# Layer 3 of a four-layer network: who empties the score banks, VectorE alone or ScalarE and VectorE crosswise

## The chip, the cores and the metric

The kernel runs on one core of one Trainium2 chip. The metric is the device time of one execution in microseconds; less is better. Five engines work side by side, each through its own queue in order: TensorE (PE, with its weight loads shown as PEld), VectorE (DVE), ScalarE (ACT), GpSimd (POOL) and SyncE (SP), which issues most of the DMAs.

## The reference

The input is `x`, 4 images of 256 channels and 48 x 48 pixels in fp32. Four layers follow each other, each a residual layer on a group norm: `x = x + layer(gn(x))`. Layer 0 is a 7x7 dilated attention, layers 1 and 2 are 3x3 convolutions with quantized weights. Layer 3, the one that is changed, is a linear attention with three window sizes:

```python
# x stands for gn(x) here
q = sigmoid(Wq x); k = sigmoid(Wk x); v = normalized(Wv x)      # 8 heads of 32 channels
Ikv = integral(k v^T)                                          # running sums over rows and columns
for w in (1, 2, 4):
    wkv = box(Ikv, 48 // w)                                    # sum over a window around each pixel
    attn = (q . wkv) / (q . box(integral(k), 48 // w) + 1e-6)
out = Wout concat(attn for each w) + bout
```

For each pixel and head, then, the products of `q` with the `k` of all pixels in a window of 48, 24 or 12 pixels a side weight the `v` of these pixels.

## The kernel before, in words

The kernel computes layer 3 as sums over masked scores. Image `b`, half of the heads `ct` (4 heads, two pairs) and a stripe of 8 rows of queries `rb` make a block; there are 4 x 2 x 6 = 48 blocks. Keys come in tiles of 8 rows by 16 columns, so that 128 keys fill the partitions: row stripe `a`, column group `c` of 3. `tiles_of(rb)` lists the tiles that the widest window reaches: those up to three stripes away. The half sizes of the three windows are `HALVES` = 24, 12 and 6, numbered `wi` = 0, 1, 2.

For each tile and each of the two pairs, `scores` has TensorE multiply 128 keys with the queries that the widest window can reach, into a tile `s` of two PSUM banks. `ps_s` holds two such tiles, one for each pair, so the next tile's scores of a pair wait until this tile's are read. `masked` then turns scores into up to three pieces in an SBUF tile `sm`, one for each window, each multiplied by a 0/1 mask (bf16, `masks`). `sums` multiplies the pieces with `v` and adds them up in the accumulators `acc`, one for each window; it runs two tiles later (`LAG = 2`), after that tile's scores. Pool `smp` has six `sm` tiles, two for each of three tiles of keys.

What `masked` does depends on how many stripes lie between keys and queries:

- Up to one stripe (`full` and `many` hold; a *near* tile, 384 of 720): the widest window covers whole columns, which `whole` adds from precomputed sums, so that only strips at its sides are masked (`pieces[0]`: one of 16 columns or two of 8). The middle window's piece (`wi` 1) is 27, 28 or 39 columns of 8 rows for two heads: 432, 448 or 624 elements per partition. VectorE multiplies strips and middle straight from PSUM. GpSimd makes the smallest window's piece out of the middle piece, in SBUF.
- Two stripes (`full`, not `many`; 192 tiles): the strips as above by VectorE; ScalarE copies the 3 or 4 rows of the middle piece to SBUF, and GpSimd masks it there in place. The two engines go crosswise: ScalarE copies the second pair while VectorE reads the first, then they change over.
- Three stripes (not `full`; 144 tiles): only the widest window reaches, and VectorE multiplies the whole piece, 560 to 768 elements, from PSUM for both pairs.

`tiles_of` takes near and far tiles in turn. The main loop's order is written out by hand and kept (`InOrder`): scores of tile n, its masking, the sums of tile n - 2, then `advance()`, which lets the background jobs take a step: the projections of the next image (`Projection`), the running sums for the norms (`k_sums`), the norms (`norms`), the states of the keys (`state`, `window_state`), and loading and finishing of blocks (`prepare`, `finish`). These put work on all engines between two tiles. Most instructions are recorded through one helper, so the profile gives them one line, L143, and they are told apart by the names of their tiles.

The order of masking before is this, with `first` and `second` the two pairs; of `copy` and `middle` at most one does something for a given tile:

```python
copy(*second)
middle(*first)
widest(*first)
copy(*first)
middle(*second)
widest(*second)
```

Of the kernel before, what the change touches and what calls it, by code (L numbers as in the profile page):

```python
# [146 lines left out]
def conv_preact_kernel(  # L147
# [53 lines left out]
    pe, dve, act, pool, sync = (  # L201
        InOrder(tc, e) for e in (nc.tensor, nc.vector, nc.scalar, nc.gpsimd, nc.sync)
    )
# [249 lines left out]
    with (  # L453
# [479 lines left out]
        def load_row(pool_, tag, a):  # L933

            t = pool_.tile([P, NCT, K0, P], F32, tag=tag, name="wrow")
            sync.dma_start(
                out=t, in_=w1[:, a * K0 : (a + 1) * K0, :].rearrange("(ct p) k o -> p ct k o", p=P)
            )
            return t
# [442 lines left out]
        with tc.tile_pool(name="wst", bufs=1) as wst:  # L1382
            for ct in range(NCT):
                fetch_x(0, ct)
            rows = [load_row(k1p, "k1", 0), load_row(vp, "v", MT), load_row(vp, "v", MT - 1)]
# [43 lines left out]
        with (  # L1429
# [11 lines left out]
            first = ExitStack()  # L1441
# [41 lines left out]
    with (  # L1483
# [243 lines left out]
        def rows_seen(wi, a, rb):  # L1727

            h = HALVES[wi]
            return (  # L1730
                max(0, a * RB - h + 1 - rb * RB),
                min(RB, a * RB + RB + h - rb * RB),
            )

        def cols_seen(wi, c):
            h = HALVES[wi]
            return max(0, c * KC - h + (wi > 0)), min(W, c * KC + KC + h)

        def rows_whole(a, rb):

            return abs(a - rb) * RB + RB <= HALVES[0]
# [5 lines left out]
        def strips(c):  # L1747

            (c0, c1), (f0, f1) = cols_seen(0, c), cols_whole(c)
            return [(p0, p1) for p0, p1 in ((c0, f0), (f1, c1)) if p0 < p1]  # L1750

        class Block:
# [28 lines left out]
            def masked(self, a, c, ss):  # L1781

                rb = self.rb
                all0 = rows_seen(0, a, rb), cols_seen(0, c)
                (r0, r1), (c0, c1) = all0
                wis = [wi for wi in range(NW) if seen(wi, a, rb)]
                full = rows_whole(a, rb)
                pieces = {wi: [cols_seen(wi, c)] for wi in wis}
                if full:
                    pieces[0] = strips(c)  # L1790

                def room():

                    t = smp.tile([P, SM_ROOM], F32, tag="sm", name="sm")
                    at, got = 0, {}
                    for wi in wis:
                        nr = rows_seen(wi, a, rb)[1] - rows_seen(wi, a, rb)[0]
                        for p0, p1 in pieces[wi]:
                            n = 2 * nr * (p1 - p0)
                            got[wi, p0] = t[:, at : at + n].rearrange(  # L1800
                                "p (j r w) -> p j r w", j=2, r=nr
                            )
                            at += n
                    assert at <= SM_ROOM
                    return got

                pairs = [room() for _ in ss]

                def view(tiles, wi, rows, cols):
                    y0, _ = rows_seen(wi, a, rb)  # L1810
                    x0 = next(p0 for p0, p1 in pieces[wi] if p0 <= cols[0] and cols[1] <= p1)
                    return tiles[wi, x0][
                        :, :, rows[0] - y0 : rows[1] - y0, cols[0] - x0 : cols[1] - x0
                    ]

                def times_mask(engine, wi, rows, cols, dst, src):
                    mr = rb * RB + rows[0] - (a * RB - HALVES[wi] + 1)
                    mc = cols[0] - (c * KC - MCOL0[wi])
                    nr, ncol = rows[1] - rows[0], cols[1] - cols[0]
                    m = mask[wi][:, mr : mr + nr, mc : mc + ncol]  # L1820
                    engine.tensor_mul(
                        dst, src, m.unsqueeze(1).to_broadcast([P, 2, nr, ncol])
                    )

                def of_banks(s, tiles, wi, rows, cols):
                    src = s[:, :, rows[0] - r0 : rows[1] - r0, cols[0] - c0 : cols[1] - c0]
                    times_mask(dve, wi, rows, cols, view(tiles, wi, rows, cols), src)

                many = seen(NW - 1, a, rb)

                def middle(s, tiles):
                    if full and many:
                        of_banks(s, tiles, 1, rows_seen(1, a, rb), cols_seen(1, c))

                def copy(s, tiles):
                    if full and not many and 1 in wis:
                        rows, cols = rows_seen(1, a, rb), cols_seen(1, c)
                        act.copy(  # L1840
                            view(tiles, 1, rows, cols),
                            s[:, :, rows[0] - r0 : rows[1] - r0, cols[0] - c0 : cols[1] - c0],
                        )

                def widest(s, tiles):
                    if not full:
                        of_banks(s, tiles, 0, *all0)
                        return
                    for cols in pieces[0]:
                        of_banks(s, tiles, 0, (r0, r1), cols)  # L1850

                first, second = zip(ss, pairs)
                copy(*second)
                middle(*first)
                widest(*first)
                copy(*first)
                middle(*second)
                widest(*second)  # L1860
                for tiles in pairs:

                    wi = NW - 1 if many else 1
                    if wi in wis:
                        rows, cols = rows_seen(wi, a, rb), cols_seen(wi, c)
                        src = view(tiles, 1, rows, cols)
                        times_mask(pool, wi, rows, cols, view(tiles, wi, rows, cols), src)
                return pairs
# [40 lines left out]
        def seen(wi, a, rb):  # L1909
            r0, r1 = rows_seen(wi, a, rb)  # L1910
            return r0 < r1
# [165 lines left out]
        for n in range(len(stream) + LAG):  # L2077
            if n < len(stream):
                i, a, c, at, last = stream[n]
# [6 lines left out]
            if n >= LAG:  # L2086
                i, a, c, at, last = stream[n - LAG]
# [60 lines left out]
```

## Time and profile before

| | before |
|---|---|
| median of 3 runs | 3681.4 us (3665.39 to 3687.82) |
| the profiled execution | 3665.04 us, span 3663.2 us |
| granted TensorE clock, mean | 0.952 |
| DVE sm<-s,masks | 2592 instructions, 1145.8 us |
| ACT sm<-s | 384 instructions, 123.4 us |
| POOL sm<-sm,masks | 1152 instructions, 822.9 us |
| PE s<-qs,ks | 5760 instructions, 870.4 us |

Layer 3's tiles run from 1388 us, where the first scores start, to 3638 us, where the last accumulator is copied. A row of the groups gives busy time and the mean of one instruction; a `sm<-s` is a product or copy that reads PSUM, `sm<-sm` one that reads and writes SBUF. A TensorE that is shown as busy need not run at its peak, since matmuls overlap: in this trace the 8 score matmuls of a tile, of 0.4 to 1.0 us each, start together and end within 0.86 us where both banks are free.

### The profile page before, as it was taken

Reading aid. Unit: us, or ns where it says so; the run is one execution under the profiler, and the core shown is the slowest. Engines: PE = TensorE matmul, PEld = TensorE weight load, DVE = VectorE, ACT = ScalarE, POOL = GpSimd, SP = SyncE. Lnnn points to the kernel's source line nnn. Section 1 sums busy time; section 2 is a strip of 40 time slices with the busy share of each in tenths; the row PEclk is TensorE's granted clock in tenths of the full one; section 3 lists DMA queues with packets and bytes.
Section 4 is the critical chain, followed back from the end, with each engine's and each line's share of the span. In section 5 each row is a group of like instructions: output and inputs, shape, how many; then the busy total and the mean of one; then the engine's idle time right before and its main releaser. Section 6 shows DMA issues by size and latency. Waiting matters only on the chain. (4 is left out here: it accounts for less than half of the span.)

```text
span 3663.2 us, 73044 instructions
## 1 busy us (share of the span) xinstructions
PE 3216.3 (88%) x28754; PEld 1942.3 (53%) x28754; DVE 2419.0 (66%) x4987; ACT 677.5 (18%) x1557; POOL 1661.6 (45%) x2548
## 2 busy tenths in 40 slices
PE   3689998998997887887899889899998899999998
PEld 2467686786785664443444444444444444444444
DVE  7976587487484365876756576765577656566664
ACT  0012111111114422222101222211222201111100
POOL 0000120030030034787876786776476777454552
PEclk9789999999998898999999999999999999999999
DMA  7746324324314423344533543344223344211222
GB/s 252 227 139 197 105 94 129 112 85 127 102 65 138 136 72 108 122 141 144 149 103 112 157 122 122 108 126 137 81 96 120 119 128 129 64 32 32 66 62 61
DMA packets 373031, 423.29 MB, mean 116 GB/s; under 512 B 129075, under 2 KB 328531, under 8 KB 371539
## 3 DMA queue, kind: packets, MB, share of 16 engines
q1 hardware_dynamic: 371491, 416.32, 36.9%
q8 instruction: 229, 3.75, 0.4%
q0 software_dynamic: 144, 1.52, 0.2%
q14 instruction: 111, 0.91, 0.1%
q10 hardware_dynamic: 1056, 0.79, 0.1%
HBM read 288.79 MB, written 131.25 MB: 115 GB/s over the span
## 5 line engine op out<-in xcount | busy, mean ns | idle before, releaser
L143 DVE TENSOR_TENSOR sm<-s,masks 128x128 f32<-128x128 f32 (+8 forms) x2592 | 1145.8, 496 | 709.7 <-PE s L143 377.7
L143 POOL TENSOR_TENSOR sm<-sm,masks 128x432 f32<-128x432 f32 (+14 forms) x1152 | 822.9, 728 | 711.3 <-DVE sm L143 512.6
L143 PE MATMUL s<-qs,ks 32*128 32x320 f32 (+3 forms) x5760 | 870.4, 505 | 109.4 <-DVE sm L143 72.5
L143 PE MATMUL acc<-sm,vs 128*32 128x64 f32 (+13 forms) x14976 | 683.0, 308 | 32.2 <-POOL sm L143 32.1
L143 PE MATMUL cv<-vx,wt 128*128 128x288 f32 x2080 | 556.9, 423 | 92.3 <-DVE vx L143 49.5
L143 PEld LDWEIGHTS s<-qs,ks 32*128 32x128 f32 x5760 | 353.1, 188 | 479.8 <-issue 195.8
L143 PEld LDWEIGHTS acc<-sm,vs 128*32 128x32 f32 x14976 | 351.0, 111 | 441.6 <-issue 269.4
L143 PEld LDWEIGHTS cv<-vx,wt 128*128 128x128 f32 x2080 | 400.5, 197 | 212.6 <-issue 55.0
L143 POOL MEMSET v<- 128x16 f32 (+1 forms) x120 | 18.6, 215 | 722.4 <-DVE vx L143 628.3
L143 ACT COPY sm<-s 128x234 f32<-128x234 f32 (+5 forms) x384 | 123.4, 343 | 915.8 <-PE s L143 784.4
L143 PE MATMUL cv<-v,wl 128*128 128x384 f32 x1152 | 224.3, 354 | 22.4 <-DVE x L143 8.6
L143 PEld LDWEIGHTS cv<-v,wl 128*128 128x128 f32 x1152 | 214.6, 195 | 32.2 <-issue 15.2
L143 POOL TENSOR_TENSOR pt<-pt 128x144 f32<-128x144 f32 x336 | 185.3, 552 | 23.4 <-DVE pt L143 0.5
L143 POOL TENSOR_TENSOR v<-l2v,v 128x384 fp32r<-128x384 f32 x96 | 109.0, 1165 | 127.4 <-ACT v L143 118.7
L143 POOL TENSOR_TENSOR nhi<-nhi,nq 128x384 f32<-128x384 f32 x144 | 144.9, 1034 | 0.3
L143 PE MATMUL cv<-pad,wl 128*128 128x384 bf16 x864 | 143.1, 327 | 0.0
L143 PE MATMUL out_ps<-o,wout_sb 128*128 128x384 f32 x288 | 124.2, 514 | 12.3 <-DMA rc<-r_d 7.6
L143 ACT COPY stage<-acc 128x384 f32<-128x384 f32 x144 | 64.0, 489 | 303.7 <-PE acc L143 272.7
L143 PE MATMUL out_ps<-stage,wout_sb 128*128 128x384 f32 x288 | 118.4, 493 | 0.7 <-DVE stage L143 0.7
L143 DVE TENSOR_TENSOR vx<-v 128x868 f32<-128x868 f32 x112 | 115.3, 1055 | 0.5
L143 PEld LDWEIGHTS <-wl 128*128 128x128 bf16 x864 | 83.9, 97 | 59.4 <-issue 0.8
L143 DVE SCALAR_TENSOR_TENSOR x<-cv,alpha,x 128x384 f32<-128x384 f32 x144 | 83.9, 610 | 41.7 <-PE cv L143 41.4
(174 smaller groups left out, 3347.4 us busy)
## 6 DMA issues: line engine op xcount, KB each, us to landing
wt<-wt SPq DMA_DIRECT2D x48, 768.0 KB
kb_d<-pt SPq DMA_DIRECT2D x48, 576.0 KB
rc<-r_d SPq DMA_DIRECT2D x192, 144.0 KB
nhi<-kb_d SPq DMA_DIRECT2D x120, 192.0 KB
nlo<-kb_d SPq DMA_DIRECT2D x88, 192.0 KB
o_d<-stage SPq DMA_DIRECT2D x24, 576.0 KB
o<-o_d SPq DMA_DIRECT2D x24, 576.0 KB
wl<-wl_d SPq DMA_DIRECT2D x16, 768.0 KB
```

The costliest lines, as they stand in the source:

```text
L143: return lambda *args, **kwargs: self.tc.keep_in_program_order(op(*args, **kwargs))
```

## The change

Near tiles: ScalarE now copies the middle piece of both pairs from PSUM to SBUF, crosswise with VectorE, which reads the strips. When both copies are made, VectorE multiplies them with the mask in place, second pair first (`again`). Tiles three stripes away: ScalarE copies the second pair's whole piece while VectorE multiplies the first pair's from PSUM; VectorE then masks the copy in place. Tiles two stripes away keep their order. The number of VectorE products does not change; 768 + 144 = 912 of them read SBUF instead of PSUM, and ScalarE gets 912 copies. The order of the instructions on TensorE, GpSimd and SyncE stays.

```diff
@@ -1830,34 +1830,43 @@
 
                 many = seen(NW - 1, a, rb)
 
-                def middle(s, tiles):
-                    if full and many:
-                        of_banks(s, tiles, 1, rows_seen(1, a, rb), cols_seen(1, c))
-
-                def copy(s, tiles):
-                    if full and not many and 1 in wis:
-                        rows, cols = rows_seen(1, a, rb), cols_seen(1, c)
-                        act.copy(
-                            view(tiles, 1, rows, cols),
-                            s[:, :, rows[0] - r0 : rows[1] - r0, cols[0] - c0 : cols[1] - c0],
-                        )
-
-                def widest(s, tiles):
-                    if not full:
-                        of_banks(s, tiles, 0, *all0)
-                        return
-                    for cols in pieces[0]:
-                        of_banks(s, tiles, 0, (r0, r1), cols)
+                def copy(s, tiles, wi):
+                    rows, cols = rows_seen(wi, a, rb), cols_seen(wi, c)
+                    act.copy(
+                        view(tiles, wi, rows, cols),
+                        s[:, :, rows[0] - r0 : rows[1] - r0, cols[0] - c0 : cols[1] - c0],
+                    )
+
+                def cut(s, tiles, wi):
+                    for cols in pieces[wi]:
+                        of_banks(s, tiles, wi, rows_seen(wi, a, rb), cols)
+
+                def again(tiles, wi):
+                    rows, cols = rows_seen(wi, a, rb), cols_seen(wi, c)
+                    t = view(tiles, wi, rows, cols)
+                    times_mask(dve, wi, rows, cols, t, t)
 
 
 
                 first, second = zip(ss, pairs)
-                copy(*second)
-                middle(*first)
-                widest(*first)
-                copy(*first)
-                middle(*second)
-                widest(*second)
+                if not full:
+                    copy(*second, 0)
+                    cut(*first, 0)
+                    again(second[1], 0)
+                elif many:
+                    copy(*second, 1)
+                    cut(*first, 0)
+                    copy(*first, 1)
+                    cut(*second, 0)
+                    again(second[1], 1)
+                    again(first[1], 1)
+                else:
+                    if 1 in wis:
+                        copy(*second, 1)
+                    cut(*first, 0)
+                    if 1 in wis:
+                        copy(*first, 1)
+                    cut(*second, 0)
                 for tiles in pairs:
 
                     wi = NW - 1 if many else 1
```

## The prediction

> **What bounds the kernel now.** I read the busy shares first, then the windows of layer 3, the waits, and two stretches of the timeline. The chain that ended last holds only the final instructions of this trace, so it carries nothing here.
>
> ```profile
> PE 3216.3 (88%) x28754; PEld 1942.3 (53%) x28754; DVE 2419.0 (66%) x4987; ACT 677.5 (18%) x1557; POOL 1661.6 (45%) x2548
> ```
>
> ```profile
> 1390.00:1900.00 510.00, 432.53 (x4642) 213.38 (x4643) 361.59 (x729) 105.18 (x264) 402.56 (x609) 0.92 0.43 130
> 1900.00:3200.00 1300.00, 1194.04 (x13166) 592.68 (x13164) 848.55 (x1829) 246.13 (x629) 879.83 (x1295) 0.98 0.39 115
> 3200.00:3640.00 440.00, 414.55 (x5085) 210.56 (x5084) 279.59 (x618) 49.55 (x151) 221.21 (x340) 0.99 0.17 51
> ```
>
> The columns after the length are PE, PEld, DVE, ACT, POOL. Over 2250 us of layer 3 PE is busy 2041 (91%), DVE 1490 (66%), POOL 1504 (67%), ACT 401 (18%). TensorE looks like the bound, ScalarE is nearly free, and VectorE and GpSimd both have a third left. Those 2250 us hold 720 tiles, 3.12 us each.
>
> ```profile
> PE s L143 <- DVE sm L143: 72.5, 205, 2.7
> PE s L143 <- ACT sm L143: 27.8, 71, 3.8
> PEld acc L143 <- POOL sm L143: 103.5, 164, 5.7
> ```
>
> Few waits are booked against the score banks, only 100 us. But TensorE also loses time that is booked as busy:
>
> ```profile
> 3253.24 0.86 PE L143 MATMUL s<-qs,ks 32*128 32x320 f32 x8 [0.34 <-ACT sm L143]
> ...
> 3254.15 1.78 DVE L143 TENSOR_TENSOR sm<-s,masks 128x432 f32<-128x432 f32 x4 [0.91 <-PE s L143]
> ...
> 3255.24 1.65 PE L143 MATMUL s<-qs,ks 32*128 32x320 f32 x8 [0.17 <-PE acc L143]
> ```
>
> One tile's scores are 8 matmuls over two pairs of heads. At 3253.24 both pairs' banks were free: 0.86 us. At 3255.24 the tile before was a near one, whose second bank VectorE released only at the end of its four products (1.78 us), so the pairs ran one after the other: 1.65 us. Counting over all 720 tiles in the trace, 320 take over 1.2 us and the mean is 1.24. After a tile two rows away, whose banks ScalarE and VectorE empty crosswise, only 13 of 192 take that long.
>
> **What the Trainium skill says.** "VectorE: DVE Perf Modes", in the tier table, keeps a two-tensor fp32 product at one element per cycle from SBUF and PSUM alike. Its errata section gives fixed costs of 58 cycles from SBUF and 120 from PSUM, 65 ns in favour of SBUF. The trace agrees with the first and not with the second: wu<-wl 128x256 from SBUF takes 421 ns, sm<-s 128x256 from PSUM 416. "SBUF — State Buffer", "SBUF: two separate sides", says that a VectorE op with two SBUF inputs and a GpSimd op exclude each other for a whole instruction. The trace agrees:
>
> ```profile
> 1564.22 0.76 DVE L143 TENSOR_TENSOR vu<-ss,vr 128x24 f32<-128x24 f32 x1
> 1565.01 0.79 DVE L143 TENSOR_TENSOR vu<-vu,vr 128x24 f32<-128x24 f32 x1
> ...
> 1567.74 1.70 DVE L143 TENSOR_TENSOR vt<-vt,vr 128x768 f32<-128x768 f32 x1
> ```
>
> ```profile
> 1564.09 1.67 POOL L143 TENSOR_TENSOR sm<-sm,masks 128x352 f32<-128x352 f32 x2
> 1565.72 2.90 POOL L143 TENSOR_TENSOR nhi<-nhi,nq 128x384 f32<-128x384 f32 x3
> 1568.59 1.91 POOL L143 TENSOR_TENSOR sm<-sm,masks 128x224 f32<-128x224 f32 x2
> ```
>
> 24 elements take 0.76 us because each product sits out a GpSimd instruction; and two GpSimd products of 224 (median 0.616 us each) take 1.91 behind vt. All medians:
>
> ```profile
> L143 POOL TENSOR_TENSOR pt<-pt x336: 482/493/1307, 1415.0 to 2940.4; 128x144 f32<-128x144 f32 x168
> L143 DVE TENSOR_TENSOR pt<-cs x144: 540/708/1381, 1409.6 to 2928.1; 128x384 f32<-128x384 f32 x144
> ```
>
> pt<-cs averages 773 ns against a least of 540: a lone product with two SBUF inputs waits 0.23 us. A product that reads s has one SBUF input and shows no such spread. "PSUM — Partial Sum Buffer", "PSUM bank collisions raise a hardware error", forbids two engines in one bank at once. That is why the two engines go crosswise; the trace shows VectorE waiting 56.6 us for ScalarE's copies.
>
> **The change part by part.**
>
> *VectorE's own work: nothing saved.* The 768 middle products stay, 205.1 + 158.2 + 153.9 = 517 us, and so do half of the 288 whole products (half of 74.4 + 66.8 + 43.9 + 39.2, 112 us). They only move their source to SBUF, at the same price alone.
>
> *ScalarE gains 912 copies.* Its sm<-s copies run from 296 ns (162) to 420 ns (312), 0.83 ns per element. Estimated from this line: 678, 532 and 519 ns for 624, 448 and 432 elements, 256 each, 443 us; the 144 whole ones about 690 ns, 100 us. ScalarE goes from 401 to about 944 us, 42% of the layer. It isn't the bound, but it now stands in the release of nearly every bank. Behind a copy queue sigmoids, stage, keys and vt copies, for which TensorE and the DMA queue wait; table loads of 1.283 us can stand ahead of one. Below I charge this nothing: between zero and 0.145 us (27.8 us over the 192 tiles that ScalarE empties now) on 528 more tiles, 77 us.
>
> *The exclusion, new.* 912 VectorE products now have two SBUF inputs. Lower end: none waits. Upper end: each waits for a mean GpSimd mask, 0.73 us, 664 us. I take 0.25 us for the first of a near tile (the lone product's figure, rounded up) and 0.40 for the second, since a GpSimd instruction that waited gets in between: 0.65 on 384 near tiles and 0.25 on 144 tiles three rows away, 286 us. VectorE comes to 1776 us, 79%. GpSimd waits in turn, an estimated 0.3 us in six cases out of ten, 164 us, to 74%.
>
> *The banks.* Take t = 0 where a near tile's scores end. Now, for a tile of 432 or 448 elements, the first bank is free at 0.7 us and the second at 1.75 (with 624: 1.0 and 2.4). After the change VectorE cuts the strips of the first pair (0.42) while ScalarE copies the second (0.53), then they swap. With 0.1 to 0.2 us for each handover both banks are free at 1.4 (1.75 with 624). So the first bank comes later and the second earlier, and the scores are no longer split. The second cut now waits for ScalarE on near tiles; behind it on VectorE stand both products in place, the layer's other work and the next tile's cuts. At most this saves TensorE 1.24 - 0.87 = 0.37 us a tile, 266 us.
>
> *VectorE's chain over a near and a far tile.* PE's work besides scores is (2041 - 893)/720 = 1.6 us a tile (893 is the sum of the score spans); VectorE's other work is (1490 - 1146)/720 = 0.48. Before: products end at 1.75 (2.4); the far scores, split in part, end at 2.6 (3.25); its banks are free at 3.65 (4.45); TensorE is ready at 4.2 (4.85) and ends the next near scores at 5.05 (5.7). Mean 5.27: TensorE decides. After: second cut ends at 1.27 (1.56); two products in place of 0.6 (0.8) and 0.65 of waits end at 3.12 (3.8); other work to 3.6 (4.3); two cuts of the far tile, 4.5 (5.45); banks free 4.6 (5.55); TensorE ready at 4.05 (4.2); next near scores end at 5.45 (6.4). Mean 5.77: VectorE decides. A far tile three rows away frees its banks faster, but its product in place then delays the next cut; I take the same 5.77.
>
> *The sum.* The layer has 360 pairs of tiles, 6.25 us each: 0.98 over the chain before, for bunched jobs and waits. With TensorE unsplit I keep 0.7 of this: 6.47, or 0.2 x 360 = 72 us more. The profiled execution of 3665.04 us (span 3663.2) would become 3737. The median of the three runs, 3681.4, lies 16 above it, so 3753: I say 3750.
>
> *Moved at no cost.* GpSimd's, SP's and TensorE's orders stay. But GpSimd's masks now start when a near tile's last product ends, 3.1 us instead of 0.75 to 1.75. TensorE wants them two tiles later, at about 6, which hides it. If GpSimd is backlogged, the 103.5 us wait of the sums' weight loads grows; that is part of the 0.7.
>
> **The rivals.** *Faster:* unsplit scores win. The chain of 5.77 leaves 0.48 of today's 6.25, 173 us; half of it gives 3595. For it: 320 split tiles, ScalarE idle. Against: VectorE gets no lighter. It decides once the two waits of a near tile sum to 0.3 us or less. *No change:* both cancel, 3680, where PE's unsplit gain and the waits meet. *Much slower:* GpSimd is always backlogged, as at 1564, and each product waits a whole instruction. The chain is 5.77 + 0.81 = 6.58, with 0.7 on top 7.28, 370 us: 4050. For it: GpSimd at 79% before 1900 us; against: 50% after 3200. *ScalarE's queue holds the banks:* with its upper 77 us, 3830.
>
> **How the numbers follow.** Slower by 1 to 5%, with ScalarE's queue counted in: 0.52; much slower 0.10; no change 0.20; faster 0.18. A measurement of this kernel can tell about 1% from no change. So slower 0.62, same 0.20, faster 0.18. The likeliest case alone spans 3720 to 3850. For 8 in 10 the range runs from the faster rival's 3600 to 3880.
>
> **What would show it.** Products sm<-sm averaging 0.2 to 0.4 us above 801, 618 and 601 ns prove the exclusion; at no excess my main cost is gone. Score spans near 0.87 us prove the unsplit gain. VectorE near 80% and PE waiting for DVE's strips make the forecast right; PE's wait for ACT copies above 100 us would mean that the ScalarE queue did it. A time under 3644 makes it wrong, and then the waits should be small or GpSimd unhurt.

## The result, and the profile after

The changed kernel takes 3816.24 us (median of 4 runs, 3808.16 to 3823.44) against 3679.52 us for the kernel before (4 runs). The ratio is 1.0375, 95% interval 1.0335 to 1.0415: 137 us slower. The profiled execution took 3823.44 us, span 3821.6. In it layer 3's tiles run from 1402 to 3798 us, 2396 us instead of 2250. So 146 of the 158 us between the two spans lie in the layer that was changed; some 14 lie ahead of it, in code that is the same.

The busy shares of the changed kernel:

```profile
PE 3142.6 (82%) x28754; PEld 1897.4 (50%) x28754; DVE 2572.2 (67%) x4987; ACT 1176.9 (31%) x2469; POOL 1847.4 (48%) x2548
```

TensorE is busy 74 us less than before, although it does the same matmuls. That goes with the unsplit scores, whose spans fall by more (180 us, below), while other matmuls take longer (the sums 313 ns on average instead of 308). VectorE is busy 153 us longer and GpSimd 186, with the same instructions in the same number. ScalarE gained 499 us; its sm<-s copies grew from 123 to 644. The windows of the layer (PE, PEld, DVE, ACT, POOL, granted clock, DMA share, GB/s):

```profile
1390.00:1900.00 510.00, 378.14 (x4111) 188.54 (x4113) 369.62 (x682) 184.81 (x404) 397.86 (x543) 0.89 0.40 122
1900.00:3200.00 1300.00, 1064.92 (x11895) 517.57 (x11888) 856.31 (x1662) 483.08 (x1041) 916.09 (x1208) 0.92 0.36 107
3200.00:3800.00 600.00, 521.39 (x6951) 263.54 (x6948) 425.50 (x855) 232.72 (x512) 375.75 (x494) 0.99 0.23 65
```

No engine is full: over these 2410 us TensorE has fallen to 82%, VectorE is at 69% and GpSimd at 70%. The groups of VectorE's products in place, by form, with busy time and mean of one in ns:

```profile
L143 DVE TENSOR_TENSOR sm<-sm,masks 128x624 f32<-128x624 f32 x256 | 225.4, 920 | 0.0
L143 DVE TENSOR_TENSOR sm<-sm,masks 128x448 f32<-128x448 f32 x256 | 203.0, 832 | 0.0
L143 DVE TENSOR_TENSOR sm<-sm,masks 128x432 f32<-128x432 f32 x256 | 185.0, 762 | 0.0
```

From PSUM the same products took 801, 618 and 601 ns. By these means they are 126 us longer together, and the whole ones of the far tiles bring it to 152 us over 912 products, 0.17 us each. (One expectation below speaks of 127 us. That figure sets busy times against each other, and in a busy time two products in place that follow directly overlap by some 0.08 us, which those from PSUM, with strips between them, don't.) The waits are uneven: the 432-element products have a least of 591 ns, a median of 601 and a longest of 1431, so that about half of them hardly wait. On GpSimd two rows of the tile `pt`, with least, median and longest duration in ns, show the other side:

```profile
L143 POOL TENSOR_TENSOR pt<-pt x336: 482/496/1307, 1428.5 to 3113.5; 128x144 f32<-128x144 f32 x168
...
L143 POOL TENSOR_TENSOR pt<-pt,carry x40: 478/858/1138, 1454.1 to 3106.7; 128x144 f32<-128x144 f32 x40
```

The least time of the second row is 478 ns and its median 858: more than half of these instructions now sit out a product of VectorE, with which they have no data in common. (Its median was 491 ns before.) In the first row the median stays (493 before), and only the mean tells: 641 ns instead of 552. And the waits (us in total, times, longest):

```profile
PEld acc L143 <- POOL sm L143: 172.6, 155, 6.2
PE s L143 <- ACT sm L143: 161.4, 271, 4.1
...
PE acc L143 <- POOL sm L143: 115.2, 89, 5.9
...
PE s L143 <- DVE sm L143: 25.4, 22, 3.6
```

Scores wait 161 us for ScalarE's copies (27.8 before) and 25 for VectorE (72.5). The matmuls of the sums wait 115 us for GpSimd's masks (32 before). A piece of the timeline in the lightly loaded last part shows one near tile:

```profile
3402.86 0.97 PE L143 MATMUL s<-qs,ks 32*128 32x384 f32 x8 [0.22 <-ACT sm L143]
...
3403.88 1.26 ACT L143 COPY sm<-s 128x624 f32<-128x624 f32 x2 [1.07 <-PE s L143]
...
3405.00 1.51 DVE L143 TENSOR_TENSOR sm<-sm,masks 128x624 f32<-128x624 f32 x2
3405.19 0.92 PE L143 MATMUL s<-qs,ks 32*128 32x320 f32 x8 [0.42 <-ACT sm L143]
...
3406.66 1.73 POOL L143 TENSOR_TENSOR sm<-sm,masks 128x270 f32<-128x270 f32 x2 [2.57 <-DVE sm L143]
```

Both pairs' next scores now run together (0.92 us), as the crosswise copies were to allow, after a wait of 0.42 us until both banks are free. GpSimd's masks begin only after the second product in place, 1.7 us after that product pair began. Over the layer 89 tiles instead of 320 take over 1.2 us for their scores, and the sum of the score spans falls from 893 to 713 us.

### The profile page after: what moved, and what is told of

Same layout as the page of the kernel before. It is cut to its first block, busy times and chain, and to the rows that moved or that the text cites. A ratio compares the mean times of both kernels' runs of the same rounds, so it can differ in the third digit from the quotient of the medians.

```text
span 3821.6 us, 74047 instructions
## 1 busy us (share of the span) xinstructions
PE 3142.6 (82%) x28754; PEld 1897.4 (50%) x28754; DVE 2572.2 (67%) x4987; ACT 1176.9 (31%) x2469; POOL 1847.4 (48%) x2548
## 5 line engine op out<-in xcount | busy, mean ns | idle before, releaser
L143 POOL TENSOR_TENSOR sm<-sm,masks 128x432 f32<-128x432 f32 (+14 forms) x1152 | 889.9, 797 | 676.8 <-DVE sm L143 516.0
L143 ACT COPY sm<-s 128x624 f32<-128x624 f32 (+6 forms) x1296 | 644.4, 521 | 1461.1 <-PE s L143 1215.1
L143 DVE TENSOR_TENSOR sm<-s,masks 128x128 f32<-128x128 f32 (+3 forms) x1680 | 608.4, 390 | 688.1 <-PE s L143 324.7
L143 PE MATMUL s<-qs,ks 32*128 32x320 f32 (+3 forms) x5760 | 696.7, 517 | 197.6 <-ACT sm L143 161.4
L143 PE MATMUL acc<-sm,vs 128*32 128x64 f32 (+13 forms) x14976 | 722.1, 313 | 116.4 <-POOL sm L143 115.2
L143 DVE TENSOR_TENSOR sm<-sm,masks 128x624 f32<-128x624 f32 (+2 forms) x912 | 756.0, 862 | 0.5 <-ACT sm L143 0.2
L143 PEld LDWEIGHTS s<-qs,ks 32*128 32x128 f32 x5760 | 270.3, 192 | 484.2 <-ACT sm L143 309.1
L143 PE MATMUL proj_ps<-wv_sb,xn 128*128 128x256 f32 x288 | 89.7, 441 | 37.4 <-ACT vt L143 21.5
L143 POOL TENSOR_TENSOR nhi<-nhi,nlo 128x384 f32<-128x384 f32 (+3 forms) x112 | 117.6, 1073 | 0.2
L143 PE MATMUL proj_ps<-xn,wq_sb 128*128 128x384 f32 x192 | 86.3, 578 | 36.4 <-ACT sg L143 26.1
```

The costliest lines, as they stand in the source:

```text
L143: return lambda *args, **kwargs: self.tc.keep_in_program_order(op(*args, **kwargs))
```

## The experiments

Four things could carry the loss: the *exclusion* of VectorE's products in SBUF and GpSimd's instructions ("the port" in two of the expectations), the *release* of the banks through two copies in series, *late masks* of GpSimd, and ScalarE's queue. Each ratio is to the kernel before, on the same chip.

**Which tiles.** E1 keeps the change on near tiles alone; this edit gives far tiles the order of before. E2 keeps the change on far tiles alone and gives near tiles the order of before:

```diff
 if not full:
-    copy(*second, 0)
     cut(*first, 0)
-    again(second[1], 0)
+    cut(*second, 0)
```

> Only the near tiles of the change; tiles three stripes away are masked by VectorE from PSUM for both pairs, as before. Three theories on the 137 us. Exclusion: the 912 products in SBUF and GpSimd's instructions shut each other out. Release: both score banks of a near tile come free only after two copies and two cuts in series, and TensorE, which then has only the sums to do, waits for ScalarE. Late masks: GpSimd starts its near masks only after the last product in place, and the sums wait for them. All three place nearly the whole loss in the near tiles: 100 to 140 us over before, ratio 1.027 to 1.038. If the far tiles matter, less than 90 us.

> Only the tiles three stripes away as changed; near tiles as before. Exclusion: 144 products wait about 0.2 us each on VectorE, which is not the bound here, so 0 to 30 us over before. Release: both banks of these tiles come free together after some 0.9 us instead of one after the other after 0.8 and 1.6, so TensorE's next scores are no longer split: 0 to 40 us under before. Late masks: no GpSimd mask in these tiles, no difference. Near 3680 us, ratio 0.99 to 1.008.

E1: 3825.73 us, 1.0412 (1.0375 to 1.045), 153 us over before. E2: 3717.76 us, 1.0135 (1.0089 to 1.0182), 45 us. The near tiles hold the loss, as all theories said, and a little more of it than the 100 to 140 us expected. The far tiles cost more than any of them said, and the two don't add up: 198 us apart, 137 together.

**Without GpSimd's near masks.** E3 is the kernel before and E4 the changed one, both with this edit; on near tiles the smallest window then goes without its mask:

```diff
 wi = NW - 1 if many else 1
 if wi in wis:
     ...
     src = view(tiles, 1, rows, cols)
+    if many:
+        tiles[wi, cols[0]] = src
+        continue
```

> The kernel before with GpSimd's masks of the smallest window left out on near tiles; the sums of that window read the middle piece. Serves as the base for the next run. GpSimd loses some 630 us of its 1504 us in the layer. The sums' waits for GpSimd (103.5 us of weight loads) shrink: 20 to 80 us under before, ratio 0.98 to 0.995, under each theory.

> The changed kernel with the same masks of GpSimd left out on near tiles. What counts is its distance to the run before it. Exclusion and late masks: without GpSimd's near masks the products in place find the port free and nothing waits for a late mask, so the distance falls from 137 us to under 50. Release: TensorE still waits for ScalarE's two copies, the distance stays at 90 us or more, and the wait of the scores for ScalarE's copies stays above 120 us.

E3: 3606.45 us, 0.9816 (0.9781 to 0.9852). E4: 3627.95 us, 0.9881 (0.9845 to 0.9918). The distance falls from 137 to 21 us, although in E4's waits the scores wait as long for the copies as in the changed kernel:

```profile
PE s L143 <- ACT sm L143: 158.6, 271, 3.8
```

So the wait for the copies alone doesn't make 137 us. GpSimd's near masks are needed for the loss. Whether they lose by being late or by shutting VectorE out is open here. One thing in E4 was not expected: the products in place don't find GpSimd out of their way. From its groups by line and its waits:

```profile
L143 DVE TENSOR_TENSOR sm<-sm,masks 128x624 f32<-128x624 f32 (+2 forms) x912 | 714.7, 817 | 0.0
...
PE acc L143 <- POOL sm L143: 15.2, 7, 4.9
```

They average 817 ns, against 862 in the changed kernel and 688 without a second input (E5, next): three quarters of VectorE's own waiting is still there, next to GpSimd's other work, and GpSimd grows by 143 us from E3 to E4. Yet only 21 us are lost, and the sums hardly wait for GpSimd (15 us instead of 115). So VectorE's waits as such are cheap there; this reads as if they cost time mainly where GpSimd, held up in turn, delivers its near masks late.

**One SBUF input instead of two.** E5 keeps order, waits and lengths of the changed kernel, and takes only the second input away; the 912 pieces go without their mask:

```diff
 def again(tiles, wi):
     rows, cols = rows_seen(wi, a, rb), cols_seen(wi, c)
     t = view(tiles, wi, rows, cols)
-    times_mask(dve, wi, rows, cols, t, t)
+    dve.tensor_reduce(t, t.unsqueeze(4), AX.X, ALU.add)
```

> The changed kernel with each of the 912 products in place replaced by a reduce over an axis of length one, which rewrites the copy without the mask: one SBUF input instead of two, same order, same waits, about the same length. Exclusion: VectorE and GpSimd no longer shut each other out over these instructions; the excess of VectorE (127 us over 912) and most of GpSimd's growth (186 us) go, and the time falls by 70 us or more, below 3745. Late masks: GpSimd still starts after the last of them, the time stays within 35 us of the changed kernel's 3816.

E5: 3658.45 us, ratio 0.9964 (0.9948 to 0.998). The whole loss is gone, and 13 us more. The busy shares of E5, and from its groups by line the rewrites:

```profile
PE 3065.9 (84%) x28754; PEld 1869.4 (51%) x28754; DVE 2405.5 (66%) x4987; ACT 1175.9 (32%) x2469; POOL 1657.5 (45%) x2548
```

```profile
L143 DVE TENSOR_REDUCE sm<-sm 128x624 f32<-128x624 f32 (+2 forms) x912 | 595.6, 688 | 0.5 <-ACT sm L143 0.2
```

The 912 rewrites take 596 us, where the products in place took 756 (means 688 and 862 ns). Their forms of 624, 448 and 432 elements average 792, 608 and 592 ns, within 10 ns of the products from PSUM, so the length is nearly the same and the waiting is gone. GpSimd's 2548 instructions, not one of them edited, fall from 1847 to 1658 us, which is the 1662 of before. Exclusion is shown, on both engines, by this run. It also clears the other three as the cause of the 137 us: release and ScalarE's queue are as in the changed kernel (ScalarE is busy 1175.9 us), and GpSimd's masks still come after the second rewrite of a tile. What these three cost and what the change gains without exclusion nets to the 13 us; and the sums wait less for the masks:

```profile
PE acc L143 <- POOL sm L143: 65.3, 57, 5.1
```

**Earlier masks.** E6 gives ScalarE's near copies buffers of their own; VectorE masks from there into `sm`, and GpSimd takes its piece from the copy without waiting for VectorE (the buffers and GpSimd's side of the edit are left out below). E7 turns GpSimd's two masks round:

```diff
-        view(tiles, wi, rows, cols),                    # copy()
+        tiles["raw"] if "raw" in tiles else view(tiles, wi, rows, cols),
...
-    times_mask(dve, wi, rows, cols, t, t)
+    times_mask(dve, wi, rows, cols, t, tiles.get("raw", t))
```

```diff
-for tiles in pairs:
+for tiles in pairs[::-1] if many else pairs:
```

> The changed kernel, but ScalarE's copies of near tiles go to a buffer of their own (two, one for each pair); VectorE writes its masked middle piece from there into sm, and GpSimd takes the smallest window's piece straight from the copy, without waiting for VectorE. Products with two SBUF inputs stay 912. Late masks: GpSimd starts some 1.2 to 1.9 us earlier, the sums' wait for it falls from 115 us to near the 32 of before, and the time falls by 70 us or more, below 3745. Exclusion: both engines now want the port at the same moment, the time stays within 35 us of 3816 or rises.

> The changed kernel with GpSimd's two near masks of a tile in the other order, second pair first, as VectorE finishes them. Late masks: the first of the two starts one product earlier (0.76 to 0.92 us), so a part of the loss goes: 20 to 60 us under 3816. Exclusion: GpSimd now runs against VectorE's last product, no gain, within 20 us of 3816, or slower.

E6: 3913.96 us, 1.0659 (1.0639 to 1.0679), slower than the changed kernel by 98 us. E7: 3816.2 us, 1.0392 (1.0376 to 1.0408), no difference from it. Neither earlier start gains anything. In E7 GpSimd is busy 1912 us instead of 1847, so the earlier start is met by more waiting. In E6 the sums wait less for GpSimd (48 us instead of 115), but the two engines hold each other up more; its groups by line:

```profile
L144 POOL TENSOR_TENSOR sm<-raw,masks 128x336 f32<-128x336 f32 (+8 forms) x768 | 800.1, 1061 | 492.4 <-DVE sm L144 251.2 <-ACT raw L144 186.4 <-issue 22.2
L144 DVE TENSOR_TENSOR sm<-raw,masks 128x624 f32<-128x624 f32 (+2 forms) x768 | 723.9, 983 | 0.0
```

VectorE's near products average 983 ns (838 in the changed kernel; 673 from PSUM). But E6 isn't clean. It has only two of the new buffers, so that ScalarE's next copy, and with it the release of a bank, waits until GpSimd has read the last one:

```profile
ACT raw L144 <- POOL sm L144: 249.7, 95, 10.7
```

In the changed kernel ScalarE's copies wait 60 us for GpSimd, and its scores 187 us for ScalarE and VectorE together; in E6 the scores wait 301. How much of the 98 us is exclusion and how much this new wait was not taken apart. That late masks are not the cause by themselves rests on E5, where their place in the order is unchanged and the loss is gone.

**Fewer or shorter products with two inputs.** E8 has ScalarE copy all of the second pair, while VectorE multiplies all of the first from PSUM. E10 copies only the second pair's strips, and E11 both pairs' strips; both leave the far tiles as before (shortened, with several statements on a line):

```diff
 elif many:
-    copy(*second, 1); cut(*first, 0); copy(*first, 1); cut(*second, 0)
-    again(second[1], 1); again(first[1], 1)
+    copy(*second, 1); strips_out(*second); middle(*first); cut(*first, 0)        # E8
+    again(second[1], 1); strips_again(second[1])
+    strips_out(*second); middle(*first); cut(*first, 0)                          # E10
+    middle(*second); strips_again(second[1])
+    strips_out(*second); middle(*first); strips_out(*first); middle(*second)     # E11
+    strips_again(first[1]); strips_again(second[1])
```

> Near tiles without crossing over: ScalarE copies all of the second pair (middle and strips), VectorE meanwhile multiplies all of the first pair from PSUM, then masks the second pair's copies in place. Products with two SBUF inputs on near tiles: 384 middle pieces and 512 strips instead of 768 middle pieces. Both banks are free after 1.1 us (1.5 with 624) instead of 1.4 (1.75), and GpSimd can begin with the first pair while VectorE works on the second. Late masks: most of the loss goes, 3680 to 3740. Exclusion: shorter products but more of them, 3740 to 3810. If unsplit scores come without either loss, it beats before: below 3640.

> The kernel before, except that on near tiles ScalarE copies the second pair's strips while VectorE multiplies the first pair; VectorE then does the second middle piece from PSUM and masks the strips in place last. The second bank comes free 0.4 to 0.55 us earlier, the first as before. 512 products with two SBUF inputs, but short ones (0.28 and 0.42 us from PSUM). Exclusion: each waits about 0.15 to 0.3 us, 75 to 150 us on VectorE, which has room; GpSimd is held shortly. If the price of exclusion goes by the length of a product, about even, 3640 to 3700; if it goes by their number, 3700 to 3760.

> As the run before, but crosswise for both pairs: ScalarE copies both pairs' strips, VectorE does both middle pieces from PSUM and then all strips in place, 1024 short products with two SBUF inputs. Both banks are free after 1.3 us (1.7 with 624) and GpSimd can start after the first middle piece. Exclusion by length of a product (0.13 and 0.27 us of data instead of 0.45 to 0.65): a third of the changed kernel's loss, 3640 to 3720. By number (1024 against 912): as slow as the changed kernel, 3780 to 3840.

E8: 3811.42 us, 1.0381 (1.0359 to 1.0403). E10: 3701.14 us, 1.0105 (1.0075 to 1.0135). E11: 3847.91 us, 1.05 (1.0473 to 1.0526). E8 lies at the upper edge of what exclusion gave, E10, 38 us over before, on the border of its two readings, and E11 a little above its range by number. The groups by line of E10 and then of E11:

```profile
L143 DVE TENSOR_TENSOR sm<-sm,masks 128x128 f32<-128x128 f32 (+1 forms) x512 | 276.1, 559 | 0.0
```

```profile
L143 DVE TENSOR_TENSOR sm<-sm,masks 128x128 f32<-128x128 f32 (+1 forms) x1024 | 624.5, 659 | 0.0
```

From PSUM the two kinds of strip average 280 and 416 ns, 348 over both. In place they average 659 in E11, 0.31 us more each, and 559 in E10, 0.21 more. The long pieces of the changed kernel lose 0.17 each. So shortening the products does not help: 1024 strips lose more than 912 long pieces. That the loss goes by number is not shown either: E11 has twice the strips of E10 and loses 185 us over before against 38, and it also changes how both banks are released. None of these versions beats the kernel before.

**What is left without exclusion.** E9 and E12 are E2 and E1 with the reduce of E5 in place of the product, so their pieces go without masks too.

> Near tiles as before; tiles three stripes away as changed, but the 144 products in place replaced by a reduce over an axis of length one, which leaves out the mask there and reads one SBUF input. Exclusion: if the 45 us that the far tiles alone cost come from these products, they go, and with the unsplit scores the time falls to before or under it: 3640 to 3685. A rival: the far tiles' cost lies in ScalarE's copy standing in its queue and holding the second bank; then it stays 30 us or more over before.

> Near tiles as changed, with the 768 products in place replaced by a reduce over an axis of length one, which leaves out their mask and reads one SBUF input; far tiles as before. If the far tiles' copies cost some 30 us by themselves and the exclusion is the near tiles' only loss, what remains is the gain of the unsplit scores: 3610 to 3645, ratio 0.985 to 0.995. If the crosswise copies gain nothing: 3655 to 3680.

E9: 3696.28 us, 1.0089 (1.0055 to 1.0124). E12: 3705.31 us, 1.0089 (1.0072 to 1.0106). Each half alone costs 31 to 34 us without any exclusion, while both together (E5) gain 13. My expectations for both were wrong: in E9 the sign of the rival, 30 us or more over before, was met. The score spans show why the halves need each other. In E12, 100 of the 143 near tiles that follow a tile three stripes away still have split scores (82 before, 28 in E5), because VectorE empties that tile's banks one after the other. In E9 it is 203 of the 336 far tiles that follow a near one (196 before, 8 in E5). E12's spans sum to 726 us against 686 in E5, and these 40 us are most of what lies between the two. But E5's own gain is small as well, since scores there still wait 139 us for ScalarE's copies. How the half that unsplits its scores (E12's spans sum to 167 us less than before) ends above before, rather than at it, I did not settle; its TensorE waits 87 us more for banks and masks (219 instead of 132), which gives back only half.

By these ratios the exclusion costs 1.0375 - 0.9964 of 3.68 ms, about 151 us, in the whole change; 1.0412 - 1.0089, about 119, in the near tiles; and for the far tiles 1.0135 - 1.0089, some 17, where the intervals overlap.

## Why the prediction was right

The time lies in the range, on the forecast side, and the mechanism named as the main cost is the one that E5 removes. The path from this cost to the time was another than forecast, though, and that the side came out right owes something to luck. Step by step:

- *VectorE saves nothing by reading SBUF:* right. The shortest product in place of 432 elements takes 591 ns, against 601 on average from PSUM, and E5's one-input rewrites match the PSUM durations to 10 ns.
- *ScalarE's copies:* right. 681, 535 and 521 ns, against estimates of 678, 532 and 519.
- *The exclusion's waits:* right in kind. On VectorE I said 286 us and 152 came (159 by the comparison with E5); a near tile's two products wait 0.33 us together, not 0.65. The excess of 0.12 to 0.21 us over the PSUM times hardly reaches the 0.2 to 0.4 that was to prove exclusion; E5 proves it. GpSimd waits 186 us, against 164. VectorE ended at 69% and not at 79%.
- *Unsplit scores:* right. Spans fell by 180 of at most 266 us, to a mean of 0.99 us instead of 0.87.
- *"VectorE decides":* not shown, and the signs speak against it. VectorE was to be near 80%, with TensorE waiting for its strips; it is at 69%, and scores wait 25 us for it, less than before. They wait for ScalarE's copies (161 us), and the sums for GpSimd's masks (115 us).
- *The sum:* mis-sized in two terms that pull against each other. (It has a slip, too: 6.47 less 6.25, over 360 pairs, is 79 us and not 72.) With the measured 0.33 in place of 0.65, my chain of 5.77 us becomes 5.45, and with 0.7 on top 6.15 a pair, 36 us *under* before. A pair of tiles takes 2396/360 = 6.66. So what stays over the chain is 1.21 us and not the 0.7 of "I keep 0.7 of this": the waiting between engines grew, where I let it shrink. The waits for GpSimd's masks and for both banks at once are where the trace books it. That the two errors left the forecast on the right side is the luck in it; 72 us were forecast and 137 came.
- *GpSimd's later masks "at about 6, which hides it":* wrong as a wait, since the sums wait 83 us more for them. As a cause by itself the later place falls: it is the same in E5, where the loss is gone.
- *The point at which the faster rival decides*, waits of 0.3 us or less: almost reached (0.33), and yet the kernel is 137 us slower. The threshold looked at VectorE's half of the exclusion alone. With both halves gone (E5) the gain is 13 us and not 85; the scores there wait 139 us for ScalarE.
- *"PE's wait for ACT copies above 100 us would mean that the ScalarE queue did it":* a bad criterion. It is 161 us in the slow kernel and 139 in E5, which is faster than before.

## What to carry to other kernels

Moving a VectorE product's source from PSUM to SBUF changes more than its address: with the mask in SBUF too it becomes an instruction with two SBUF inputs, and here GpSimd's products in SBUF, masks and background work alike, were then its rivals. Before such a move, look for an instruction of that kind already in the trace and compare its mean with its least time (the median can hide the waits: 601 ns against a mean of 762 for the 432-element products). Don't count on shorter instructions waiting less. And price the other engine too: here GpSimd, without one edited instruction, lost more time than VectorE did, and E4 suggests that the waits are dear mainly where another engine's work is behind them.

## What the runs showed that I had not expected

Short instructions with two SBUF inputs wait more each than long ones: 0.31 us for strips of 128 and 256 elements (E11), which come two to four in a row, against 0.17 for pieces of 432 to 768, of which at most two do. Whether the row is the reason was not tried apart. And the granted TensorE clock goes with the gaps: from 1900 to 3200 us it was 0.98 before, 0.92 in the changed kernel, 0.96 in E5 and 0.92 in E6, whose TensorE is the idlest of the four. Sums of the same shapes averaged 308 ns before, 313 after and 308 in E5. Which of the two brings about the other was not tried; if the slower clock is what lengthens the sums, the same 1.5% over the 1964 us that TensorE is busy in the layer would be some 30 us of the loss, as an estimate.
